# A four-layer graph attention kernel: tile 0 of the second layer computed densely, dense passes by halves of the heads, masks gathered as whole rows

## The chip, the cores and the metric

The kernel runs on one core of one Trainium2 chip. Time is device microseconds of an execution, here the median of three runs. The engines in the profile are PE (TensorE), DVE (VectorE), ACT (ScalarE), POOL (GpSimd) and SP (SyncE, which issues plain DMAs). Each has its own instruction queue and works it off in order; semaphores tie the queues together.

## The reference

Four graph attention layers run on 3327 nodes with 512 features and one symmetric adjacency matrix that holds about 16 neighbours per node, the node itself included. In each layer

```
h = relu(layernorm(x))
V = h W                                   # H heads of D = 512 / H features
e[i, j] = leaky_relu(s_i + d_j, 0.2)      # s, d: V times two vectors, per head
alpha = softmax over the neighbours j of i
x = x + act(sum_j alpha[i, j] V[j])       # act: elu in layers 1 and 2, else identity
```

with H = 8, 4, 1 and 8 heads in layers 0, 1, 2 and 3. (Below, "layer 1" is the second layer.) The nodes are padded to 26 tiles of 128.

## The kernel before, in words

**Preparation.** For each of the 26 row tiles the kernel loads the adjacency rows, finds each node's neighbours (up to 40, as sorted indices `L`), ranks the nodes by degree, and computes layer 0's rows of V (264 columns in each of two halves of the heads: 256 features and 8 score columns). Rows go to a table in DRAM: `tabx` for layer 0 (V and x side by side), `tab0` and `tab1` in turn for the others. The last part sorts nodes by degree into tiles: tile 0 holds the nodes with most neighbours. `CAPS` gives each tile's number of neighbour columns, from 36 (tile 0) down to 11 (tile 25), 467 in all. `Slots` holds the table indices of every tile and column. If the graph doesn't fit these caps, another branch (`tile_gat_dense`) runs; it didn't here.

**Lists.** In `tile_gat_lists` most tiles are computed from lists. A step is a group of up to four columns of one tile. `Tile.fetch` (L784 inside `gather`) issues one indirect DMA on POOL per column, which brings 128 table rows of 2112 B; in layers 1 to 3 the tile's own row comes through SP from `own_d` (L815). `scored` adds the scores and takes the exp (L839 to L842). `group` multiplies every gathered row by its weight on DVE (L865, 128x512) and adds the products up on PE with an identity matmul (L870, two records per product). In layer 2, with its one head, DVE does both (L858, L860) and PE is left to the dense passes. `finish` divides by the sum of weights, and `ends` lays out what follows over the next steps: `bent` (elu on ACT, L893 and L895), `added`, `centre`, `root`, `turn` (transposes, L451), `cut` (relu out of PSUM, L458), `project` (L469), `rows` (scaling, L476, and a write to `own_d`), and `scatter` (L792, one indirect DMA on POOL per tile).

**Dense passes.** The tiles of highest degree can be computed against all 26 source tiles j instead: a weight for every pair of nodes, times a mask, times V. `DENSE = [0, 0, 9, 2]` says how many tiles that is per layer. In layer 2 `Wholes` takes tiles 0 to 8 in three passes of three. In layer 3 `Several` takes tiles 0 and 1 with all 8 heads: for each j it loads 264 KB of the table (`ve`) and a mask (`mk`), ACT turns the mask into bf16 (L1157), PE copies it to PSUM (L1159), ACT computes three exps (L1161 to L1165) and eight Relus (L1171), DVE scales the features (`features`, L1176) and masks the weights (`masked`, L1185, two of 1024 elements), and PE multiplies (`products`, L1197).

**Masks.** They are made in layer 0 for tiles 0 to 8. A `Mask` step gathers half an adjacency row per node (6656 B, two gathers per tile), ACT makes it bf16 (L983), PE transposes it in pieces of at most 7 blocks (L989), ACT writes bytes (L995) and SP stores them.

**Order.** The order of PE, DVE, ACT and POOL is written by hand (`manual_schedule`). The loop over steps s runs `fetch` for the step that lies LOOK = 7 ahead, then the pieces registered by `later` for "first", then `scored` of step s + 1, the pieces for "scored", `group` of step s, and the pieces for "last". Tiles go from 25 down to the lowest list tile, and `place` spreads the pieces of the dense passes over the steps. `gpool` has seven buffers of four gathered rows, `mpool` three. In PSUM each tile of layers 0, 1 and 3 takes two banks of pool "o" in turn (four buffers): one for its sum `po`, one for its weights `pw`. Pool "t" (transposes) has two buffers in layers 0 and 1.

## Time and profile before

| | |
|---|---|
| median of three runs | 3105.87 us (3096.56 to 3113.53) |
| the profiled execution's own time | 2579.0 us |
| its span | 2577.0 us, mean granted clock 0.934 |
| preparation, up to the first gather | 274 us |
| layer 0, first to last gather | 274 to 925 us |
| layer 1 | 957 to 1530 us |
| layer 2 | 1560 to 2010 us, then a tail to 2050 us |
| layer 3 | 2051 to 2556 us |
| gathers and scatters of layers 0, 1 and 3 (POOL instructions) | 510, 457 and 406 |
| bytes moved | 613.85 MB, mean 238 GB/s |

The profiled execution is 527 us shorter than the median of the runs, which carry no trace. All rows of the trace belong to the shorter one.

How to read the trace: one row is a group of instructions of one line, with its engine, operation and tiles (out<-in), their number, busy time and mean duration; after a bar comes the idle time of the engine just before them and who ended it. "issue" stands for a wait that the profile shows no other engine for. A matmul's own duration overlaps with its neighbours', so a run of them is priced by the length of the run. Layers were cut by the times of their first and last gathers.

### The profile page before, as it was taken

What the parts mean: (1) busy time and instruction counts of PE and PEld (TensorE: products, weight loads), DVE (VectorE), ACT (ScalarE), POOL (GpSimd) and SP (SyncE); (2) the same over time, 40 slices, a digit from 0 to 9 for tenths busy, and PEclk for the clock granted to TensorE, in tenths of its full rate; (3) what the DMA queues carried; (4) which work ended last, traced back from release to release, by engine and by line L of the source; (5) the groups of instructions that cost most, each with busy time, mean ns of one, the idle gap of its engine ahead of it and who ended that gap; (6) DMA issues with size and microseconds to landing.
All of it is one profiled execution on the core that took longest, in us unless ns stands there. A gap on an engine that the chain in (4) does not pass through costs nothing. (4 is left out here: it accounts for less than half of the span.)

```text
span 2577.0 us, 25558 instructions
## 1 busy us (share of the span) xinstructions
PE 2113.2 (82%) x6708; PEld 1154.2 (45%) x6708; DVE 1965.1 (76%) x5080; ACT 756.5 (29%) x1827; POOL 1806.9 (70%) x1818
## 2 busy tenths in 40 slices
PE   3677799988988858998898986768787599998988
PEld 2566345444434424544444432435443445454543
DVE  8988887776666637888777765897989488878777
ACT  4876033223222201222211112343342322222221
POOL 6996477777777747777777764665656277777775
PEclk7898899999999989999999997888898799999999
DMA  5884688888888858888888785886878288888886
GB/s 227 306 321 177 193 257 265 267 282 262 262 266 259 244 155 236 247 243 240 237 236 238 235 220 191 262 251 222 253 234 249 99 251 245 250 243 243 242 239 178
DMA packets 234928, 613.85 MB, mean 238 GB/s; under 512 B 79059, under 2 KB 83155, under 8 KB 231446
## 3 DMA queue, kind: packets, MB, share of 16 engines
q0 software_dynamic: 135216, 464.80, 60.2%
q1 hardware_dynamic: 95814, 140.54, 16.1%
q10 hardware_dynamic: 3744, 6.82, 0.8%
q8 instruction: 54, 0.88, 0.1%
q14 instruction: 100, 0.82, 0.1%
HBM read 545.12 MB, written 66.89 MB: 237 GB/s over the span
## 5 line engine op out<-in xcount | busy, mean ns | idle before, releaser
L870 PE MATMUL bank<-m,ident 128*128 128x512 f32 x2680 | 1253.3, 615 | 201.6 <-DVE m L865 179.2
L865 DVE TENSOR_TENSOR m<-g,bank 128x512 f32<-128x512 f32 x1340 | 832.4, 681 | 103.5 <-ACT bank L842 97.9
L784 POOL DMA_INDIRECT g<-tab,idxb x769 | 733.0, 953 | 251.9 <-issue 180.5
L870 PEld LDWEIGHTS bank<-m,ident 128*128 128x128 f32 x2680 | 500.8, 195 | 836.8 <-DVE m L865 399.1
L469 PE MATMUL pv<-w,hT 128*128 128x264 f32 x1664 | 430.6, 415 | 80.9 <-ACT hT L458 58.1
L469 PEld LDWEIGHTS pv<-w,hT 128*128 128x128 f32 x1664 | 335.8, 205 | 183.8 <-ACT hT L458 73.4
L842 ACT ACTIVATE bank<-z 128x32 f32<-128x32 f32 (+4 forms) x371 | 71.8, 194 | 1169.4 <-DVE z L841 1169.1
L784 POOL DMA_INDIRECT g<-tabx,twiceb x342 | 324.5, 949 | 104.2 <-issue 78.6
L784 POOL DMA_INDIRECT g<-tab,idxa x297 | 282.7, 952 | 106.6 <-issue 69.5
L1076 PE MATMUL whole<-ve,em 128*128 128x512 f32 x468 | 224.5, 631 | 27.3 <-DVE em L1062 26.6
L839 DVE TENSOR_TENSOR z<-g,bank 128x32 f32<-128x32 f32 (+4 forms) x371 | 65.2, 176 | 217.5 <-DMA g<-tabx,twiceb 84.4
L628 POOL TENSOR_TENSOR key<-a,keys 128x3328 int32<-128x3328 int32 x26 | 189.3, 7290 | 4.3 <-DMA a<-in_adj 3.4
L860 DVE SCALAR_TENSOR_TENSOR bank<-g,pw,bank 128x512 f32<-128x512 f32 x243 | 183.2, 754 | 6.8
L1076 PEld LDWEIGHTS whole<-ve,em 128*128 128x128 f32 x468 | 92.4, 202 | 135.5 <-issue 105.1
L635 DVE MAX8 cand<-key 128x8 f32<-128x208 int32 x416 | 143.7, 364 | 0.6 <-POOL key L628 0.6
L451 PE MATMUL pt<-ident,xn 128*128 128x128 f32 x416 | 69.3, 293 | 88.1 <-ACT hT L458 36.1
L784 POOL DMA_INDIRECT g<-tabx,twicea x99 | 95.0, 960 | 61.7 <-issue 26.8
L792 POOL DMA_INDIRECT tab<-v,idxb x54 | 53.7, 994 | 101.9 <-ACT v L476 86.7
L451 PEld LDWEIGHTS pt<-ident,xn 128*128 128x128 f32 x416 | 53.4, 150 | 132.9 <-issue 44.5
L1197 PEld LDWEIGHTS whole<-vs,em 128*128 128x128 f32 x832 | 101.1, 189 | 25.0 <-issue 23.8
L1051 ACT ACTIVATE r<-low,mc,b 128x384 f32<-128x384 f32 x78 | 52.6, 675 | 167.7 <-DVE em L1062 150.9
L1197 PE MATMUL whole<-vs,em 128*128 128x130 f32 x832 | 101.4, 274 | 0.0
(168 smaller groups left out, 1920.3 us busy)
## 6 DMA issues: line engine op xcount, KB each, us to landing
a<-in_adj SPq DMA_DIRECT2D x26, 1664.0 KB, 9.3
ve<-tab SPq DMA_DIRECT2D x104, 264.0 KB, 4.5
own<-v SPq DMA_DIRECT2D x78, 264.0 KB, 3.8
g<-own SPq DMA_DIRECT2D x67, 264.0 KB, 4.1
tabx<-vx SPq DMA_DIRECT2D x26, 528.0 KB, 3.9
g<-tab,idxb POOLq DMA_INDIRECT x769, 3.9
vx<-in_x ACTq DMA_DIRECT2D x26, 256.0 KB, 2.8
g<-tabx,twiceb POOLq DMA_INDIRECT x342, 4.1
```

The lines of the kernel that those rows point to most:

```text
L451: nc.tensor.transpose(pt[:, k, :], xn[:, k * P:(k + 1) * P], ident)
L469: nc.tensor.matmul(pv[:, s, :HF + 8], hT[:, k, :], W.w[:, k, s, :], start=(k == 0), stop=(k == KC - 1))
L628: nc.gpsimd.tensor_tensor(key, a, keys, OP.mult)
L635: nc.vector.max(cand[:, g * 8:(g + 1) * 8], key[:, g * SEG:(g + 1) * SEG])
L784: nc.gpsimd.indirect_dma_start(out=out_, out_offset=None, in_=table, in_offset=bass.IndirectOffsetOnAxis(ap=which, axis=0))
L839: nc.vector.tensor_tensor(z, g[:, :n, ROW - 8:ROW - 8 + H], self.s.unsqueeze(1).to_broadcast([P, n, H]), OP.add)
L842: nc.scalar.activation(self.wt[:, k0:k0 + n, :H], z, AF.Exp)
L860: nc.vector.scalar_tensor_tensor(acc, v, w, acc, OP.mult, OP.add)
L865: nc.vector.tensor_tensor(m[:, q, :].rearrange("p (s h d) -> p s h d", s=2, d=D), v.rearrange("p s (h d) -> p s h d", d=D), wt[:, k0 + q, ...
L870: nc.tensor.matmul(self.po, ident, m[:, q, :], start=(k0 + q == 0), stop=(k0 + q == K - 1))
L1076: nc.tensor.matmul(tl.po.rearrange("p (s m) -> p s m", s=2), e[:, q * P:(q + 1) * P], v.rearrange("p (s m) -> p s m", s=2)[:, :, :F // 2], ...
L1197: nc.tensor.matmul(dst, e[:, h - 4 * half, q * P:(q + 1) * P], mov, start=False, stop=(j == NT - 1), skip_group_check=True)
```

## The change

It has these parts.

1. `DENSE[1]` becomes 1: in layer 1 tile 0 is no longer gathered column by column but goes through `Several`, with masks that exist already.
2. `Several` is rewritten. A unit is one source tile j and one half of the heads (2 of 4 in layer 1, 4 of 8 in layer 3), so a layer has 52 units; all 26 j of the upper half come first. Each unit loads its half of the table rows (132 KB) and the mask (16 KB for one tile, 32 KB for two). ACT writes the Relus into PSUM (`r`, one buffer) and scales the features, one instruction per head; DVE multiplies by the mask's bytes as they are, so that the bf16 mask and its copy by PE fall away. Loads are issued three units ahead. Its buffers are cut (`Room`) out of `low`, `L` and `spare`, which lie free after the preparation, and, for two tiles, one more.
3. A mask step gathers the whole adjacency row (13312 B) of each node into `low`: one gather per tile, steps 11 apart instead of 7 per half; one conversion of 3328 elements; four pieces of turning, whose copies stand in "last" instead of "scored".
4. PSUM: pool "o" has two buffers and holds only sums; weights lie in banks of their own, two in layer 0, and the two halves of one in layers 1 and 3. Pool "t" has one buffer.
5. `cut` moves from ("scored", b + 3) to ("last", b + 2), just after `turn`; in layer 2 `rows` moves from b + 5 to b + 4. `place` gets n - 8 steps instead of n - 6.
6. `Own` is for a dense tile in layer 0 and isn't used with this `DENSE`.

The diff, cut to its core:

```diff
-DENSE = [0, 0, 9, 2]
+DENSE = [0, 1, 9, 2]
...
-                                    (b + 2, "first", self.turn), (b + 3, "scored", self.cut),
-                                    (b + 3, "last", self.project), (b + 5, "scored", self.rows),
+                                    (b + 2, "first", self.turn), (b + 2, "last", self.cut),
+                                    (b + 3, "last", self.project), (b + 5 - (HEADS[self.l] == 1), "scored", self.rows),
...
     class Mask:
...
         def fetch(self):
-            n = NP // 2
-            g = gpool.tile([P, GROUP, ROW], F32, name="g")
-            self.a = g.rearrange("p q n -> p (q n)")[:, :n].bitcast(I32)
-            if self.side:
-                nc.scalar.activation(odd[:, self.t:self.t + 1], slots(self.t, 0, twice=True), AF.Copy, bias=1.0)
-            gather(self.a, adj.rearrange("r (s n) -> (r s) n", s=2),
-                   odd[:, self.t:self.t + 1] if self.side else slots(self.t, 0, twice=True))
+            self.a = low.bitcast(I32)
+            gather(self.a, adj, slots(self.t, 0))
...
         def finish(self, s):
-            for i, (c0, c1) in enumerate([(0, 7), (7, NT // 2)]):
+            for i, c0 in enumerate(range(0, NT, 7)):
+                c1 = min(c0 + 7, NT)
                 later(s + 1 + i, "first", self.turn(c0, c1))
-                later(s + 1 + i, "scored", self.keep(c0, c1))
+                later(s + 1 + i, "last", self.keep(c0, c1))
...
     class Several:
...
-        def features(self, j):
-            H, D, n = self.H, self.D, self.n * P
-            v = self.v.pop(j).rearrange("p (s m) -> p s m", s=2)[:, :, :F // 2]
-            nc.vector.tensor_tensor(
-                self.vs[j % 2][:, :H * (D + 1)].rearrange("p (s h d) -> p s h d", s=2, d=D + 1)[:, :, :, :D],
-                v.rearrange("p s (h d) -> p s h d", d=D),
-                self.k[j][:, n:n + H].rearrange("p (s h) -> p s h", s=2).unsqueeze(3).to_broadcast([P, 2, H // 2, D]),
-                OP.mult)
+        def load(self, u):
+
+            if u < 2 * NT:
+                i, j = divmod(u, NT)
+                table = tabs[self.l % 2] if self.l > 0 else tabx
+                c0 = (1 - i) * (ROW // 2)
+                nc.sync.dma_start(self.v[u % 3], table[j * P:(j + 1) * P, c0:c0 + ROW // 2])
+                nc.sync.dma_start(self.mk[u % 3], masks[0][j, :, :self.n * P])
+
+        def weights(self, u):
+
+            if u == 2 * NT:
+                return
+            i, j = divmod(u, NT)
+            n, Q, H, D = self.n * P, self.Q, self.H, self.D
+            if i == 0:
+                d = self.v[u % 3][:, ROW // 2 - 8:ROW // 2 - 8 + H]
+                nc.scalar.activation(self.b[:, j, :], d, AF.Exp, scale=1.0 - SLOPE)
+                nc.scalar.activation(self.c[:, j, :], d, AF.Exp, scale=SLOPE)
+            r = pools["r"].tile([P, self.n, BANK], F32, name="r").rearrange("p a b -> p (a b)")
+            self.r = r[:, :Q * n].rearrange("p (h c) -> p h c", h=Q)
+            for h in range(Q):
+                g = (1 - i) * Q + h
+                nc.scalar.activation(self.r[:, h, :], self.a[:, g, :], AF.Relu, bias=-1.0,
+                                     scale=self.b[:, j, g:g + 1])
+
+        def features(self, u):
...
+            for h in range(Q):
+                nc.scalar.activation(vs[:, h, :D], self.v[u % 3][:, h * D:(h + 1) * D], AF.Copy, scale=c[:, h:h + 1])
+            nc.scalar.activation(vs[:, :Q, D], c, AF.Copy)
+
+        def masked(self, u):
+            Q, n = self.Q, self.n * P
+            nc.vector.scalar_tensor_tensor(self.e[u % 2], self.r, 1.0,
+                                           self.mk[u % 3].unsqueeze(1).to_broadcast([P, Q, n]), OP.add, OP.mult)
...
+        def place(self, s0, s1):
+
+            later(s0 - 1, "first", self.begin)
+            for u in range(3):
+                later(s0 - 1, "first", lambda u=u: self.load(u))
+            later(s0 - 1, "scored", lambda: (self.weights(0), self.features(0)))
+            for u in range(2 * NT):
+                s = s0 + u * (s1 - s0) // (2 * NT)
+                later(s, "first", lambda u=u: self.masked(u))
+                later(s, "scored", lambda u=u: (self.weights(u + 1), self.features(u + 1), self.load(u + 3)))
+                later(s + 1, "first", lambda u=u: self.products(u))
+                if u % NT == NT - 1:
+                    later(s + 1, "last", lambda u=u: self.means(u // NT))
...
-            pools = {"o": pool("ps_o", 1 if whole else 4, **psum)}
+            pools = {"o": pool("ps_o", 1 if whole else 2, **psum)}
             if l < NL - 1:
-                pools.update(t=pool("ps_t", 1 if whole else 2, **psum))
+                pools.update(t=pool("ps_t", 1, **psum))
...
+                pools.update(p=pool("ps_p", 1 if DENSE[l] else 2, **psum))
                 if DENSE[l]:
-                    pools.update(w=pool("ps_w", 3, **psum), k=pool("ps_k", 1, **psum), e=pool("epool", 1))
+                    pools.update(w=pool("ps_w", l // 3 + 1, **psum), r=pool("ps_r", 1, **psum))
...
             if l == 0:
-                for i, (t, side) in enumerate(itertools.product(range(ND), range(2))):
-                    steps.insert(12 + 7 * i, (Mask(t, side), 0))
-            if DENSE[l]:
-                wholes.place(len(steps) - 6)
+                for t in range(ND):
+                    steps.insert(18 + 11 * t, (Mask(t), 0))
...
+            if whole:
+                wholes.place(len(steps) - 8)
+            elif DENSE[l]:
+                wholes.place(32 if l == 0 else 0, len(steps) - 8)
```

## Prediction

> **What bounds the kernel now.** I read the page first (busy shares, then the groups), next the busy times cut at the layers' edges, then the waits of layer 1, and last the instructions around layer 2's end. The page's first part says only that no engine is full, because it averages over stages:
>
> ```profile
> span 2577.0 us, 25558 instructions
> PE 2113.2 (82%) x6708; PEld 1154.2 (45%) x6708; DVE 1965.1 (76%) x5080; ACT 756.5 (29%) x1827; POOL 1806.9 (70%) x1818
> ```
>
> Cut at the layers' edges (start:end, length, then PE, PEld, DVE, ACT, POOL busy with instructions, granted clock, DMA share, GB/s; the rows are layers 0, 1, 2, the gap after 2, and 3):
>
> ```profile
> 274.00:930.00 656.00, 570.18 (x1702) 284.57 (x1702) 465.53 (x1232) 160.34 (x349) 485.91 (x510) 0.96 0.85 256
> ...
> 956.00:1530.00 574.00, 505.34 (x1381) 254.14 (x1382) 438.89 (x1165) 113.06 (x297) 434.38 (x457) 0.97 0.80 237
> ...
> 1560.00:2010.00 450.00, 335.46 (x948) 186.08 (x948) 371.54 (x711) 161.31 (x395) 271.07 (x287) 0.86 0.76 239
> 2010.00:2050.00 40.00, 24.99 (x96) 19.06 (x96) 14.13 (x33) 12.05 (x24) 7.55 (x9) 0.83 0.18 68
> 2050.00:2560.00 510.00, 462.85 (x1690) 252.71 (x1691) 408.03 (x847) 130.45 (x428) 385.44 (x406) 0.98 0.82 243
> ```
>
> POOL looks like the third engine, but divide length by its instructions: 574/457 = 1.256 us in layer 1, 510/406 = 1.256 us in layer 3. A constant pitch through tiles of 11 and of 36 columns means that something issues without pause. The waits of layer 1 (total, times, longest) say what:
>
> ```profile
> POOL g L784 <- issue: 97.8, 321, 0.3
> ```
>
> The longest is 0.3 us and no engine is awaited: each gather is 0.95 us and is followed by a fixed 0.30. So POOL's issue of indirect DMAs, 1.25 us each, sets layers 0, 1 and 3; its 75.6% is its ceiling. PE is next (505 of 574 = 88% in layer 1). Layer 2 is different: DVE has 372 of 450 there, and a tail in which it has ended and nothing is gathered:
>
> ```profile
> 2022.66 0.75 DVE L883 TENSOR_SCALAR low<-bank,den 128x512 f32<-128x512 f32 x1
> ...
> 2028.29 0.60 ACT L458 ACTIVATE hT<-pt 128x512 f32<-128x512 f32 x1 [3.98 <-PE pv L469]
> ...
> 2034.04 0.62 ACT L893 ACTIVATE neg<-low 128x512 f32<-128x512 f32 x1
> ...
> 2047.41 1.03 POOL L792 DMA_INDIRECT tab<-v,idxb  x1 [6.32 <-ACT v L476]
> ```
>
> The last tile's mean is ready at 2023.4, yet ScalarE takes it up at 2034.0: in its order three hT and three v of earlier tiles stand ahead, most of them waiting for a PE projection. That is 10.6 us on the path.
>
> **What the Trainium skill says.** *DMA: Bandwidth & Descriptors*, SWDGE vs HWDGE vs iDMA: descriptors of a DMA issued on GpSimd are generated in software on its cores. The trace agrees that the price is per gather, not per byte: 0.942 us for a half adjacency row (6656 B), 0.943 for a double table row (4224 B), 0.953 for one row (2112 B). *ScalarE: Activation LUTs*, What ACT_TABLE_LOAD costs: 186 ns + 0.833 ns per element, 93 more for a pointer operand, 93 of overlap between neighbours. The trace has 495 ns for the 256-wide Relu of L1171 (the formula gives 493); I use it for widths that the trace lacks. *PSUM — Partial Sum Buffer*, bank collisions: two engines must not touch one bank at once. This bears on the two tiles' scores that now share a bank; the trace already shows m waiting 0.3 us for the next group's exp in its own bank.
>
> **The change, part by part** (against the profiled execution: 2579.0 us, of it 2577.0 span).
>
> 1. *Layer 1, tile 0 without lists.* POOL loses 35 gathers (36 columns; the own row came through SP): 35 x 1.25 = 43.8 us on the path. What is late next? PE: out go 36 x 2 records at 0.43 (8 in 3.43 us on the chain) = 30.9; in come 52 units x 2 heads x 2 records at 0.112 (16 in 1.79) = 23.3, zeroing 2 banks 1.7, targets 2.1. So 505.3 - 30.9 + 27.1 = 501.5 in 574 - 44 = 530, 94.6%. The stretch 1000 to 1100 us already has 94.4% PE with POOL at full pitch, so I keep the gain, minus 3 us for the first small tiles, where PE's work per tile is about POOL's time. DVE: out 36 x 0.62 = 22.3, nine groups of z 3.1, divisors 1.2; in 52 masked products of 256 elements at 0.49 (line through 384 at 0.610 and 1024 at 1.211) = 25.5: level, 439 of 530. ACT: per unit two Relu and two scalings of 128 (387 - 93 = 294 ns each, estimate from the ScalarE page), two copies or exps of about 0.2: 1.6, so 83; 113 + 83 - 2 = 194 of 530, covered. SP gets 104 loads at 0.32 us of issue, three units (some six steps of 5 us) ahead against 3.6 to 4.5 us to landing; behind them stand the own-row loads, with seven steps of lead. Bytes: 36 x 264 KB = 9.5 MB out, 52 x (132 + 16) KB = 7.7 MB in. **-41 us.** Ends: -44 if PE never stops POOL; about -4 if PE keeps all of its 69 idle us (501.5 + 69 = 570).
>
> 2. *Masks from whole rows (layer 0).* Eighteen gathers become nine: 9 x 1.25 = 11.3 us. No row shows a gather of 13312 B per partition. From below 0.95, since three sizes up to 6656 B cost alike; from above twice that, if it cost like two halves, with nothing gained. I take 0.95, for the three rows are flat. The same bytes in bigger lumps make list rows behind them land late: the 1664 KB loads of the same rows land in 9.3 us, the halves in 6.8; POOL, up to seven steps ahead, doesn't wait for landing. ACT's conversion is one piece of about 3 us instead of two of 1.58, with a step of 5 us as cover; uncovered, 9 x 1.5 = 14 us. One PSUM buffer for turning instead of two makes PE wait for ScalarE's copy (0.9 us) when a mask and a tile turn in one step; PE's 13% of idle covers it. **-11 us.**
>
> 3. *Layer 3 by halves.* POOL's list is unchanged, 406 instructions: **0**. DVE loses 26 x 0.685 = 17.8 us, PE 26 k products (7.1), ACT gains 26 x 2 x (4 x 0.24 + 0.19) - 26 x 0.6 = 44 (24%), none of it on the path at 80%, 91% and 26%. ACT's old wait for PE's k (67.8 us in all) goes too, into idle time. SP gets 52 more issues. Uncovered, ACT's 44 is the loss.
>
> 4. *Layer 2's order.* cut follows turn in the same step, rows come a step earlier, and the dense passes are placed over n - 8 steps instead of n - 6: the last pass ends at step 60 instead of 63, while the last list tile still finishes at 71. In the changed order only one v stands between ScalarE's last exp and the last neg, where there were three hT and three v. Of the 10.6 us I take 9, as that v may wait for PE. DVE has the same work. Ends: 0 to -13 (with part of PE's 21.5 us of waits for hT inside the layer). **-9 us.**
>
> 5. *Scores in halves of one bank (layers 1 and 3).* At each of 49 tile changes m or exp may wait 0.3 us: 15 us in all, hidden in DVE's idle time (91 us left in layer 1, 120 in layer 3): 0, at most 15. The zero column, Room and the idle class Own: 0.
>
> Sum -41 - 11 + 0 - 9 = -61: the profiled execution should go from 2579 to about 2518. The median, 3105.87, is 527 us (1.204 times) above that execution and the page doesn't say where they lie. I subtract the sum unscaled: 3106 - 61 = **3045 us**; scaled it is 73 and 3033.
>
> **Rivals.**
> - *PE takes over in layer 1*: for it, 94.6%; against it, the stretch with 94.4% at full pitch. -4 - 11 - 9 = -24: 3082.
> - *The unprofiled time stretches POOL's issue*, or layer 2 gives its 13 as well: -73 to -92: 3014 to 3033, say 3030.
> - *The extra 527 us belong to something that the change doesn't relieve* (DMA time: layer 1 loses 1.8 MB, layer 3 gains 0.8 in shorter rows): only the tail remains, 3097. The profile can't speak against it.
> - *Slower: ScalarE's new bundle* (1.6 us per unit in layer 1, 2.9 in layer 3: Relus, scalings, copies) stands in one queue ahead of the next group's exp, and scaling waits for PE to leave vs. An exp has one step, 5.0 us, of lead; from a bundle plus wait above 5 us on, every unit stops m, and with it the buffers that gathers need. If half of each bundle shows, 52 x 0.8 + 52 x 1.45 = 117: 3106 - 61 + 117 = 3162. Against it: ACT at 37% and 34%, and m's own buffers bind on PE first.
>
> **How the numbers follow.** Forecast 0.50 (own range 3033 to 3058); stretched POOL 0.14; PE 0.16; unrelieved 0.12; slower 0.08. A measurement of this kernel can tell about 0.5% (15.5 us) from no change. Faster 0.50 + 0.14 + 0.16 = 0.80, same 0.12, slower 0.08. The range runs from 3012 (stretched) to 3090 (PE rival with the mask gather at double price, which returns another 11) and leaves out the last two.
>
> **What would show it.** Layer 1 near 533 us with some 422 POOL instructions at a pitch of 1.256; a pitch of 1.33 or more there and POOL waiting for DVE m means PE took over. Layer 0 some 11 us shorter, nine gathers into low at about 0.95 us; 1.9 would refute step 2. Layer 3 at 510 with ACT near 175. Between DVE's last mean in layer 2 and the next gathers about 19 us instead of 28. I am wrong if POOL gets waits longer than 0.3 us in layers 0, 1 or 3, or if profile and median move by different amounts.

## The result and the profile after

The changed kernel takes 2982.15 us (2978.08 to 2986.43, four runs), the kernel before 3108.05 beside it: ratio 0.960, interval 0.957 to 0.963, a gain of 126 us. I had forecast 3045, a gain of 61. The sign was right and the gain was twice what I had summed.

The profiled execution of the changed kernel took 2978.08 us, as long as its other runs, while that of the kernel before, from which my sum was made, took 2579.0. The experiments point to the reason: **the two traces were taken on chips of two kinds.** On four of the chips used below the kernel before takes 2578 to 2587 us, on three others 3105 to 3124, and on each of them its profiled execution, where it was taken, agrees with its other runs. I call them quiet and stopping chips, for a reason that follows. By its time, the trace of before belongs to the first kind; the forecast's runs and the trace of after belong to the second. Which chips these first runs had is not on record, and each later chip was used for one group of runs only, so it stays open whether the kind belongs to the chip or to the time of the runs. So the trace of after answers to mine only through two more traces: after on a quiet chip (e3) and before on a stopping one (e14).

The first part of the page, after on the forecast's chip:

```profile
span 2976.4 us, 26618 instructions
...
PE 2249.4 (76%) x6832; PEld 1233.1 (41%) x6832; DVE 1939.2 (65%) x5056; ACT 890.3 (30%) x2321; POOL 1771.0 (60%) x1774
```

POOL has lost 44 instructions, 35 gathers and nine halves of masks, as summed. But POOL is now at 60% where before it was at 70%. Busy times cut at the layers' edges show where the span went (start:end, length, then busy us and instructions of PE, PEld, DVE, ACT, POOL, granted clock, DMA share, GB/s; rows are layers 0 to 3). First a quiet chip, the kernel before (e4), then after (e3), on the same one:

```profile
275.00:949.00 674.00, 586.03 (x1740) 292.64 (x1740) 474.02 (x1259) 163.29 (x355) 485.93 (x510) 0.96 0.83 250
956.00:1569.00 613.00, 531.91 (x1454) 269.12 (x1454) 455.40 (x1205) 118.56 (x309) 443.99 (x467) 0.97 0.78 228
1572.00:2045.00 473.00, 350.24 (x1024) 199.34 (x1024) 382.99 (x730) 170.47 (x413) 277.29 (x295) 0.88 0.73 230
2048.00:2567.00 519.00, 470.68 (x1708) 255.78 (x1708) 414.21 (x859) 130.54 (x429) 386.40 (x407) 0.98 0.80 240
```
```profile
273.00:938.00 665.00, 582.88 (x1740) 294.38 (x1740) 474.32 (x1260) 162.13 (x337) 477.06 (x502) 0.96 0.83 253
945.00:1512.00 567.00, 515.07 (x1604) 280.89 (x1604) 447.37 (x1202) 200.19 (x613) 410.94 (x432) 0.98 0.81 244
1516.00:1972.00 456.00, 347.76 (x1029) 196.39 (x1027) 383.40 (x730) 170.46 (x415) 277.20 (x294) 0.87 0.76 239
1978.00:2498.00 520.00, 462.32 (x1652) 246.30 (x1652) 402.67 (x837) 179.15 (x632) 388.86 (x407) 0.98 0.81 241
```

Then the stopping chips, the kernel before (e14), then after (the forecast's own run):

```profile
277.00:1105.00 828.00, 626.17 (x1740) 311.18 (x1740) 472.54 (x1259) 161.53 (x355) 485.45 (x511) 0.88 0.69 203
1113.00:1848.00 735.00, 572.84 (x1454) 286.59 (x1454) 453.15 (x1205) 119.69 (x309) 442.37 (x466) 0.88 0.66 190
1852.00:2355.00 503.00, 365.55 (x1024) 203.58 (x1024) 383.57 (x730) 170.83 (x413) 277.55 (x295) 0.85 0.70 216
2358.00:3105.00 747.00, 531.43 (x1708) 281.23 (x1708) 415.56 (x859) 130.43 (x429) 386.59 (x408) 0.84 0.57 166
```
```profile
276.00:1104.00 828.00, 622.49 (x1740) 311.43 (x1738) 472.01 (x1260) 162.04 (x337) 477.54 (x501) 0.88 0.68 203
1112.00:1823.00 711.00, 562.96 (x1604) 298.85 (x1604) 447.10 (x1202) 201.43 (x613) 409.86 (x431) 0.89 0.67 195
1827.00:2312.00 485.00, 358.04 (x1030) 201.36 (x1029) 383.83 (x730) 170.32 (x413) 278.31 (x294) 0.86 0.73 224
2318.00:2972.00 654.00, 519.60 (x1652) 272.89 (x1652) 398.86 (x837) 180.97 (x632) 390.32 (x408) 0.86 0.66 191
```

Read the lengths, and then how little the busy times of DVE, ACT and POOL differ between the kinds of chip: the work is the same, only the waiting and TensorE's clock are not. From the exact start of each layer's first gather to that of its last scatter (a little more than the front's cut, which ends with the gathers):

| us | quiet: before | after | gain | stopping: before | after | gain | forecast |
|---|---|---|---|---|---|---|---|
| layer 0 | 674.1 | 664.5 | 9.6 | 827.8 | 828.3 | -0.5 | 11 |
| layer 1 | 612.5 | 566.8 | 45.7 | 735.9 | 711.3 | 24.6 | 41 |
| layer 2 with its tail | 472.3 | 456.6 | 15.7 | 502.6 | 485.6 | 17.0 | 9 |
| layer 3 | 518.6 | 520.5 | -1.9 | 746.1 | 653.9 | **92.2** | 0 |
| preparation and joints | 289.6 | 289.8 | -0.2 | 292.3 | 292.4 | -0.1 | 0 |

The gains add up to 69 us on the quiet chip, where the timed runs give 70, and to 133 on the stopping ones, where they give 126 (the two traces there are of two chips). So my sum holds where its trace came from, and most of what it missed lies in **layer 3**, which I had put at nothing.

**What a stopping chip does.** First what POOL waits for in layer 1 of after, on the forecast's chip and then on the quiet one (total, times, longest):

```profile
POOL g L786 <- issue: 109.7, 347, 1.1
...
POOL g L786 <- DVE m L865: 42.8, 21, 9.1
```
```profile
POOL g L786 <- issue: 93.5, 307, 0.3
```

On the quiet chip no "issue" wait of a gather exceeds 0.3 us, as before the change, and the gathers keep their pitch of 1.258 us; on the other the pitch is 1.55 us. There POOL stands up to 9.1 us behind DVE's m, which is what I had named as the sign that I am wrong. Behind DVE's waits stands TensorE, often by way of ScalarE: in layer 3 of after, on the forecast's chip, DVE's m waits for ScalarE's exp up to 25.7 us, and ScalarE's scaling of the features for TensorE's products up to 12.0. TensorE's matmul records in that layer, on the same chip (start, length, instruction, idle before it):

```profile
2776.26 1.02 PE L1233 MATMUL whole<-spare,low 128*128 128x130 f32 x7
2779.81 0.77 PE L870 MATMUL bank<-m,ident 128*128 128x512 f32 x1 [2.53 <-issue]
2783.31 1.01 PE L870 MATMUL bank<-m,ident 128*128 128x512 f32 x1 [2.73 <-issue]
2785.41 1.01 PE L870 MATMUL bank<-m,ident 128*128 128x512 f32 x1 [1.08 <-issue]
2787.50 1.01 PE L870 MATMUL bank<-m,ident 128*128 128x512 f32 x1 [1.09 <-issue]
```

Records that follow each other in 0.43 us elsewhere start 3.50, 2.10 and 2.09 us apart: multiples of 0.70, with "issue", no other engine, as their releaser. I call this a stop: for some 12 us TensorE starts only four of these records, and then goes on. The granted clock follows it (start:end, length, then the columns as above):

```profile
2777.00:2780.00 3.00, 0.47 (x3) 0.20 (x2) 2.93 (x7) 0.00 (x0) 2.18 (x3) 1.00 0.83 227
2780.00:2789.00 9.00, 3.70 (x5) 0.96 (x4) 1.04 (x3) 2.03 (x5) 4.52 (x5) 0.51 0.71 209
```

In the first 3 us TensorE is busy for 0.47 and the clock is still 1.00; only then does it fall. In layers 0 and 3 of this trace gathers start over 4 us apart about every 30 us (28 times in 828 us, 20 in 654); on the quiet chip once and never. Counting sequences of at least four TensorE records (products and weight loads) that start 0.70 us or a small multiple apart gives 19 in the after trace, 12 in e14's and 24 in e16's; in each of the traces from quiet chips, none. The count finds the long, regular stops only.

Why I don't take the half clock for the cause: the Trainium skill, *TensorE: Matmul & The Clock Gate*, Part 1 (The HAM clock gate), says that the array falls to half clock after an idle window of about 3.4 us, and that its activity gate knows half and full clock only. The traces agree: their clock records hold 0.5 and 1.0 alone, in pieces of 3.41 us or a multiple (but for the last, which the end of the trace shortens). e5, with fewer products, fell from 0.938 to 0.872 without losing time, so a low mean clock alone is no loss. And imposed stops make layer 3's gain on a quiet chip whose mean clock is 0.95 (e7 and e8 below). How much of the longer time on a stopping chip the half clock adds was not separated.

### The profile page after: what moved, and what is told of

It reads as the page before. It is cut to its first block, busy times and chain, and to the rows that moved or that the text cites. A ratio compares the mean times of both kernels' runs of the same rounds, so it can differ in the third digit from the quotient of the medians.

```text
span 2976.4 us, 26618 instructions
## 1 busy us (share of the span) xinstructions
PE 2249.4 (76%) x6832; PEld 1233.1 (41%) x6832; DVE 1939.2 (65%) x5056; ACT 890.3 (30%) x2321; POOL 1771.0 (60%) x1774
## 5 line engine op out<-in xcount | busy, mean ns | idle before, releaser
L870 PE MATMUL bank<-m,ident 128*128 128x512 f32 x2608 | 1320.9, 655 | 322.3 <-DVE m L865 189.4
L865 DVE TENSOR_TENSOR m<-g,pw 128x512 f32<-128x512 f32 x1304 | 810.9, 681 | 535.3 <-ACT pw L842 309.4
L870 PEld LDWEIGHTS bank<-m,ident 128*128 128x128 f32 x2608 | 525.9, 209 | 973.8 <-issue 631.1
L786 POOL DMA_INDIRECT g<-tab,idxb x734 | 701.7, 956 | 376.5 <-issue 199.8
L469 PE MATMUL pv<-w,hT 128*128 128x264 f32 x1664 | 450.7, 429 | 82.3 <-ACT hT L458 42.4
L842 ACT ACTIVATE pw<-z 128x32 f32<-128x32 f32 (+5 forms) x434 | 83.3, 192 | 878.1 <-DVE z L841 454.4
L839 DVE TENSOR_TENSOR z<-g,pw 128x32 f32<-128x32 f32 (+5 forms) x434 | 74.3, 171 | 102.8 <-DMA g<-tab,idxa 63.0
L458 ACT ACTIVATE hT<-pt 128x512 f32<-128x512 f32 x104 | 61.1, 588 | 200.0 <-remote 111.6
L476 ACT ACTIVATE v<-pv,rstd 128x528 f32<-128x528 f32 x78 | 54.2, 695 | 210.7 <-PE bank L870 104.5
L1210 ACT ACTIVATE spare<-room,low 128x64 f32<-128x64 f32 x208 | 57.8, 336 | 183.8 <-remote 81.7
```

Source lines behind the costliest of these rows:

```text
L458: nc.scalar.activation(hT, pt, AF.Relu)
L469: nc.tensor.matmul(pv[:, s, :HF + 8], hT[:, k, :], W.w[:, k, s, :], start=(k == 0), stop=(k == KC - 1))
L786: nc.gpsimd.indirect_dma_start(out=out_, out_offset=None, in_=table, in_offset=bass.IndirectOffsetOnAxis(ap=which, axis=0))
L839: nc.vector.tensor_tensor(z, g[:, :n, ROW - 8:ROW - 8 + H], self.s.unsqueeze(1).to_broadcast([P, n, H]), OP.add)
L842: nc.scalar.activation(self.wt[:, k0:k0 + n, :H], z, AF.Exp)
L865: nc.vector.tensor_tensor(m[:, q, :].rearrange("p (s h d) -> p s h d", s=2, d=D), v.rearrange("p s (h d) -> p s h d", d=D), wt[:, k0 + q, ...
```

## Experiments

**e0, e4, e11, e14: the kernel before again,** for its trace on other chips. No edit.

> The kernel before, unchanged, for a second trace beside its median of 3108. Theory A (one of two courses of the same program was caught in the first trace, and timed executions take the other): this trace has a span near 3100, and layers 0, 1 and 3 are longer in it while the preparation is the same, about 274 us. Theory B (the 527 us lie outside the span, ahead of the first or after the last instruction): the span is again near 2577.

> The kernel before, unchanged, for its trace on the chip of this call. Theory A: if it takes about 3100 us here, the granted clock in layers 0, 1 and 3 is 0.86 to 0.89 instead of 0.96 to 0.99, half-clock spells sum to over 700 us instead of 340, and the gathers' pitch is 1.25 us outside the stalls that follow those spells; if it takes about 2587, the clock is near 0.93 again. Theory B (the lost time is in DMA or in POOL's issue): at 3100 us the pitch of the gathers is longer everywhere, or the DMA's packets take longer.

> The kernel before, unchanged, on the chip of this call, for its trace. On a chip where it takes about 3106 us: TensorE's stops of 4 to 16 us (records 0.70 us apart or a multiple of it) appear in layers 0, 1 and 3 about every 28 us, as in after's forecast trace, and half-clock time is over 750 us; if they came from the changed kernel alone, they are missing here. On a chip where it takes about 2580: no such records, and a clock near 0.93.

> The kernel before, unchanged, for its trace. On a slower chip (about 3110 us): TensorE's stops as in the changed kernel's forecast trace, but more of them or longer, since the clock of its runs there (0.85 to 0.87) stands for 810 to 940 us of half clock against 758 in the changed kernel; layer 1, where the change takes 72 accumulation records out, should hold the larger part of the extra 56 us. If the stops cost both alike, each layer is longer by the same factor, 1.18 to 1.2, and the extra is spread. On another chip: 2575 to 2590 us and no stops.

Measured 2588.3 (clock 0.937), 2576.5 (0.936), 2581.8 (0.937) and 3113.8 us (0.859). The first three are quiet chips. Profiled executions and timed ones take the same on all four, so a profile doesn't shorten a run, and I take the 527 us that I had called unprofiled for the difference between two kinds of chip. The e14 trace has the stops in the kernel before too, so they aren't brought by the change. It refutes two guesses of its expectation: the extra gain is neither in layer 1 nor spread evenly.

**e1: after with tile 0 of layer 1 in lists; e2: after with masks from half rows.**

```diff
-DENSE = [0, 1, 9, 2]
+DENSE = [0, 0, 9, 2]
```
```diff
...
-                for t in range(ND):
-                    steps.insert(18 + 11 * t, (Mask(t), 0))
+                for i, (t, side) in enumerate(itertools.product(range(ND), range(2))):
+                    steps.insert(12 + 7 * i, (Mask(t, side), 0))
```

> The changed kernel with DENSE = [0, 0, 9, 2]: tile 0 of layer 1 is in the lists again, all other parts of the change stay. Theory P (the gain is the 35 gathers and their work that layer 1 loses, and POOL or PE sets it): this kernel gives back most of the 126 us, some 44 to 75, so 3026 to 3057. Theory Q (the gain is in the order and the PSUM pools, which let the queues wait less for one another in all layers): it gives back 10 to 35 only, 2992 to 3017, and layers 0 and 3 stay as in the changed kernel.

> The changed kernel with masks gathered as two half rows again (18 gathers into the ring of seven buffers, 18 conversions, steps 7 apart; the copies stay in last). Theory P (POOL's issue sets layer 0): +11 us, 2993. Theory Q (POOL isn't the bound in the timed course): within 10 us of 2982, or more than +25 if the mask steps take buffers from the ring that the lists need.

Measured on one quiet chip, against 2587.3: e1 2560.6 (ratio 0.990, 0.987 to 0.993), e2 2523.5 (0.977, 0.974 to 0.980). By layers, e1 has layer 1 at 614.4, so tile 0 is worth 47 us against e2's 567.5 on the same chip (48 against e3's 566.8). e2 has layer 0 at 676.4, so whole rows are worth 10 us against e1's 666.7 (12 against e3's 664.5). In e1's time all parts but tile 0 together give 27 us, the whole rows included.

**e3: after itself on a quiet chip; e5 and e15: after with fewer accumulations; e6: with more.** e5 and e15 leave out about half of the columns of the sums and e6 counts some twice, so their output is not the layer's; only their time is used. The edit of e5 and e15:

```diff
             for q in range(n):
+                if q % 2 and k0 + q < K - 1:
+                    continue
                 nc.tensor.matmul(self.po, ident, m[:, q, :], start=(k0 + q == 0), stop=(k0 + q == K - 1))
```

> The changed kernel itself, beside the kernel before on one chip. Theory A (my sum was right for a chip on which POOL's issue is the bound, and the extra gain of the forecast runs belongs to a chip whose TensorE clock is throttled more): where the kernel before takes about 2587 us with a granted clock of 0.93, after takes 2515 to 2525 (e2, all but the whole-row masks, was 2523.5, and nine gathers less are worth up to 11 us: 2513), so a gain of 62 to 75 us; where the kernel before takes about 3106 us, after takes about 2982, a gain of about 125, at a clock near 0.87 for both. Theory B (the extra gain is a property of the change and not of the chip): a gain of about 125 us on any chip.

> After, with every second accumulation by the identity matrix (line 870) left out in layers 0, 1 and 3, so those sums lack about half of their columns; DVE's products, gathers and everything else stay. TensorE loses about half of 1304 accumulations of 0.86 us, some 540 us of 2250 (2100 on the faster chip). Theory A (TensorE's throttled clock is what stops the buffers, and then POOL): on a throttled chip the time falls from 2980 to 2500 or less, and half-clock time to under 350 us; on the faster chip it falls from 2518 to 2470 to 2500 (stalls of TensorE in layer 1 go, POOL's 1.25 us pitch stays). Theory B (DMA or POOL): within 1% of after on either chip.

> After, with the first accumulation of each group of four columns (line 870) done twice in layers 0, 1 and 3, so those sums count some columns twice; about 330 more accumulations of 0.86 us, 280 us more for TensorE and nothing more for any other engine. Theory A: TensorE becomes the bound on any chip; on the faster chip the time goes from 2518 to 2700 or more, with more half-clock time, and POOL waits for DVE's m in stalls of some us, as on the throttled chip. Theory B: TensorE's idle time (17 to 24% of the span) takes most of it, and the time rises by under 100 us.

> The changed kernel with every second accumulation by the identity matrix (line 870) left out in layers 0, 1 and 3, as in e5. On a slower chip: if the stops follow TensorE's work (its load over some tens of us), they nearly vanish, and the time falls from 2980 to 2510 to 2600; if they come at fixed times whatever TensorE does, it stays above 2800. On another chip: 2507 us as e5, since TensorE isn't the bound there.

e3 took 2508.9 us, ratio 0.973 (0.969 to 0.976), a gain of 70 us: theory A's side, though below its 2515 to 2525. e5 (one run) took 2507.4, nothing less, though TensorE's busy time fell from 2089 to 1810: on a quiet chip TensorE isn't the bound, and A's 2470 to 2500 was too low. e6 (one run) took 2623.0: 245 us more of TensorE cost 114, between both theories, so the margin is thin there. e15 (one run), on a stopping chip, took 2932.8 against after's 2982 on the forecast's. TensorE was busy for 1894 us instead of 2249, and POOL still stood idle for over 4 us 66 times in the four layers, 67 times in after (11 in e3): the stops stayed with a sixth less work on TensorE, so the claim that they nearly vanish with its load fell.

**e7 and e8: both kernels with imposed stops; e12 and e13: with longer ones.** Products of a column of zeros are added to the group's bank, so sums stay as they are.

```diff
...
+            if 0 < k0 and next(beat) % 5 == 4:
+                for _ in range(7):
+                    nc.tensor.matmul(self.po, ident, zero.to_broadcast([P, F]), start=False, stop=False)
             for q in range(n):
...
```

e12 and e13 have 14 products there, and seven more in layer 2's dense passes:

```diff
...
+                for _ in range(7 if j % 5 == 2 and q == 0 else 0):
+                    nc.tensor.matmul(tl.po, ident, zero.to_broadcast([P, F]), start=False, stop=False)
```

> The kernel before with stops put into TensorE: in layers 0, 1 and 3, ahead of every fifth group's accumulations (about every 25 us), seven products of a column of zeros are added to the group's bank, 14 matmul records of 0.43 us, 6 us each; 59 such bursts, 354 us of TensorE. It imitates what the trace of the slower chip shows, where TensorE nearly stops for 4 to 16 us about every 28 us in those layers. Theory A (what the slower chip adds is TensorE's stops, which POOL cannot make up at a pitch of 1.25 us, and the changed kernel can absorb more of them because its layer 1 has fewer of the products that wait): on a chip where before takes 2580, this takes 2800 to 2930, and e8 gains 90 us or more on it. Theory C (stops cost both kernels alike, and the 126 us are the chip's longer time with nothing of the change in it): the gap to e8 is 70 us, as without bursts, plus at most the 12 us of the two bursts fewer.

> After with the same bursts (57 of them, 342 us). Theory A: 2700 to 2820 on a chip where after takes 2509, and a gain of 90 us or more on e7, towards the 126 of the forecast's chip. Theory C: a gain of 70 to 82 us on e7.

> The kernel before with stops twice as long: in layers 0, 1 and 3 fourteen added products of zeros (12 us) at every fifth group, 59 of them, and in layer 2 seven (6 us) at every fifth neighbour block of each dense pass, 15 of them; 800 us of TensorE in all. Theory A (stops cost the kernel before more once they are as long as the slower chip's): 3050 to 3200, and over 100 us more than e13. Theory D (stops of a given number and length cost both alike, and TensorE then sets the time, where the two kernels differ by 26 us of busy time and two stops): 30 to 75 us more than e13.

> After with the same long stops (57 of 12 us and 15 of 6 us, 774 us of TensorE). Theory A: 2930 to 3080, over 100 us less than e12. Theory D: 30 to 75 us less than e12, of it up to 24 from the two stops fewer.

Measured 2746.1 and 2684.3 us (quiet chip), 3354.7 and 3267.4 (this one a stopping chip, before 3123.8). All four totals miss what I expected, and so do the gaps: 62 us lies under theory C's 70 to 82, 87 us between D's 75 and A's 100. Cut by layers, in one trace each, they say more:

| us | e7 | e8 | gap | e12 | e13 | gap |
|---|---|---|---|---|---|---|
| layer 0 | 712.3 | 717.4 | -5 | 906.2 | 928.8 | -23 |
| layer 1 | 654.4 | 647.5 | 7 | 805.3 | 805.6 | 0 |
| layer 2 | 475.3 | 460.9 | 14 | 525.8 | 522.0 | 4 |
| layer 3 | 603.2 | 565.4 | **38** | 823.9 | 717.4 | **107** |

The more TensorE stops, the less the change gains in layers 0 and 1, where POOL's list no longer sets the time, and the more it gains in layer 3. So theory A fails for the whole kernel: by the totals the stops of e7 and e8 cost the kernel before 167 us and the changed one about 175 (2684.3 less e3's 2508.9, on another quiet chip). In layer 3 alone they cost the kernel before more. There DVE's wait for ScalarE's k grows in the kernel before with the stops: 18 us in all on a quiet chip (e4), 88 in e7, 202 in e14, 230 in e12, where the change gains -2, 38, 92 and 107 us.

**e9: three tiles without lists in layer 3; e10: dense passes over n - 6 steps.**

```diff
-DENSE = [0, 1, 9, 2]
+DENSE = [0, 1, 9, 3]
```
```diff
...
-                wholes.place(len(steps) - 8)
+                wholes.place(len(steps) - 6)
```

> After with three tiles instead of two without lists in layer 3. POOL loses the 22 gathers of tile 2, 27.5 us at 1.25; TensorE gains 52 units x 4 heads x 2 records x 0.112 = 47 and loses 23 x 2 x 0.43 = 20, so 454 + 27 = 481 of the 473 us that POOL's list would then leave in layer 3. If TensorE takes over there, as one of my rivals had it for layer 1: -15 to +20 us against after; if not: -27. Against the kernel before a ratio of 0.963 to 0.98.

> After with layer 2's dense passes placed over n - 6 steps again instead of n - 8; cut and rows stay as after has them. If the place is what opens the queue at layer 2's end (my step 4): the gap between layer 2's last DVE mean and layer 3's first gathers grows by some 5 to 9 us and the time rises to 2514 to 2520 against 2509 where before takes 2579. If cut and rows did it: within 3 us of after, a ratio of 0.972 to 0.974 to before. On a chip where before takes 3106: about 2990.

e9 took 2489.8 us, ratio 0.966 (0.964 to 0.969): layer 3 at 494.5 instead of 520.5, 26 of the 27.5 us of POOL's gathers. It beats both kernels on a quiet chip; on a stopping one it wasn't run. e10 took 2507.3, ratio 0.972 (0.970 to 0.975): after's time, with layer 2 at 460.3 us, where traces with n - 8 have 456.6 (e3) to 461.9 (e1). But its trace has the queue at layer 2's end back:

```profile
1957.11 0.75 DVE L883 TENSOR_SCALAR low<-bank,den 128x512 f32<-128x512 f32 x1
...
1969.30 0.62 ACT L893 ACTIVATE neg<-low 128x512 f32<-128x512 f32 x1
...
1985.17 1.00 POOL L786 DMA_INDIRECT g<-tab,idxa  x1 [2.62 <-issue]
```

ScalarE takes the last mean up 11.4 us after its end, and the next gathers come 27.3 us after it, as in the kernel before (e4: 12.2 and 27.6; e3: 0.03 and 18.0). In return the last mean is ready sooner: 436.7 us after the layer's first gather, against 444.0 in e3 and 448.5 in e4. So the place does open the queue, as my step 4 had it, and pays for it inside the layer; it is worth little or nothing. By elimination the gain, some 12 us in e10, comes from the order of cut and rows. TensorE's waits for ScalarE's hT in layer 2 point the same way: 63 us in e4, 25 in e10, 27 in e3. Which of the two moves does it wasn't separated.

**e16: the kernel before without TensorE's k in layer 3; e17: the same with the stops of e7.**

```diff
...
-            mk = self.mk[j] = pools["e"].tile([P, self.n * P], U8, name="mk", bufs=2)
+            mk = self.mk[j] = pools["e"].tile([P, self.n * P], U8, name="mk", bufs=3)
...
-            real = pools["e"].tile([P, n], BF16, name="real", bufs=2)
-            nc.scalar.activation(real, self.mk.pop(j), AF.Copy)
-            k = self.k[j] = pools["k"].tile([P, BANK], F32, name="k")
-            nc.tensor.matmul(k[:, :n], ident_b, real, start=True, stop=True)
+            k = self.k[j] = pools["e"].tile([P, 8], F32, name="kf", bufs=3)
...
-                                           self.k[j][:, :n].unsqueeze(1).to_broadcast([P, 4, n]), OP.add, OP.mult)
+                                           self.mk[j].unsqueeze(1).to_broadcast([P, 4, n]), OP.add, OP.mult)
```

> The kernel before with one part of the change alone, in layer 3: TensorE's product k (line 1159), which brought the mask into a PSUM bank, and ScalarE's conversion ahead of it are gone; the mask is read by DVE as it was loaded, and the factors of the features lie in SBUF; DVE still scales the features. Nothing else differs. If TensorE's k in DVE's path is what made layer 3 longer under TensorE's stops: on a slower chip (before about 3110 us) 40 to 95 us less than before, layer 3 at 650 to 705 instead of 746; on another chip within 10 us of before (2579), layer 3 near 519. If something else of the change did it (ScalarE's scaling, halves, fewer DVE instructions): within 15 us of before on either chip.

> The same edit with the bursts of e7 (59 stops of 6 us). Layer 3 was 603 us in e7 (kernel before) and 565 in e8 (changed kernel), on a chip that stops little by itself. If k in DVE's path is the cause: layer 3 at 560 to 580 and about 2710 to 2725 in all on such a chip, against e7's 2746; if not: layer 3 at 595 to 605 and 2740 to 2750.

Against "nothing else differs", the edit also gives the mask a third buffer, and the factors, which shared k's one bank, three buffers of their own in SBUF. Both runs fell on a stopping chip. e16 took 3007.3 us against 3105.2: ratio 0.967 (0.960 to 0.974), 98 us, just beyond the 40 to 95 that I expected. By layers it is e14, on another stopping chip, with one number changed:

```profile
281.00:1106.00 825.00, 626.39 (x1740) 307.95 (x1740) 472.88 (x1259) 161.92 (x355) 485.93 (x510) 0.88 0.69 204
1113.00:1846.00 733.00, 573.06 (x1454) 286.03 (x1454) 453.20 (x1205) 119.47 (x309) 442.70 (x466) 0.88 0.66 191
1850.00:2352.00 502.00, 364.18 (x1024) 204.04 (x1024) 383.72 (x730) 170.81 (x413) 277.59 (x295) 0.84 0.70 217
2355.00:3000.00 645.00, 504.75 (x1682) 278.07 (x1682) 412.30 (x859) 119.46 (x402) 408.96 (x407) 0.86 0.66 193
```

Layer 3 is 645 us where e14 has 747 and after 654. Twenty-six products of 0.27 us (median; 0.42 at most) and as many conversions of 0.40, taken out of the path, are worth the whole of layer 3's gain; ScalarE's scaling, the halves and DVE's 17.8 us are not needed for it. Of the edit's own parts the extra buffers are the untested rival. The e14 trace speaks against them: ScalarE's conversion of the mask never waits there, and TensorE waits 6.5 us in all just ahead of its 26 products k, none of it for DVE or ScalarE to leave the bank. On a quiet chip the edit wasn't run. e17 took 3071.6, with layer 3 at 671.9; its counterpart e7 ran on a quiet chip, so it decides nothing.

How so small an instruction does that is to be seen in e14, the kernel before, at one stop in layer 3:

```profile
2493.24 0.40 ACT L1157 ACTIVATE real<-mk 128x256 bf16<-128x256 uint8 x1
...
2496.68 1.01 PE L870 MATMUL bank<-m,ident 128*128 128x512 f32 x1 [1.51 <-issue]
...
2499.47 1.01 PE L870 MATMUL bank<-m,ident 128*128 128x512 f32 x1 [1.78 <-issue]
...
2508.34 0.42 PE L1159 MATMUL k<-real,ident_b 128*128 128x256 bf16 x1
...
2508.80 0.18 ACT L1161 ACTIVATE k<-ve 128x8 f32<-128x8 f32 x1 [15.16 <-PE k L1159]
...
2509.01 0.69 DVE L1176 TENSOR_TENSOR vs<-ve,k 128x512 f32<-128x512 f32 x1 [13.20 <-ACT k L1161]
```

The mask is converted at 2493.6. Its product stands in TensorE's queue behind accumulations that a stop spreads over 14 us. ScalarE waits 15.16 us for it: its exps don't use the mask, but their factors go into the same bank. DVE waits 13.20 us for ScalarE, and behind DVE's `features` stand the m of the list tiles. So after the stop TensorE soon runs out of m and stands a second time: 1.02 us at this stop, 169 us in 23 waits over layer 3. DVE's waits over layer 3, e14 and then the same kernel on a quiet chip:

```profile
DVE vs L1176 <- ACT k L1161: 201.8, 22, 13.2
```
```profile
DVE vs L1176 <- ACT k L1161: 18.4, 11, 3.6
```

In after there is no such product. DVE reads the mask as it was loaded, and the idle time of TensorE for DVE's m in layer 3 falls from 169 us (e14) to 16; in e16 it is 12. Its "issue" waits there rise at the same time, from 39 us to 112 and 120, so the stops themselves stay.

## Why the prediction missed

1. *Layer 1, tile 0: -41.* Right on a quiet chip: layer 1 gains 46, and tile 0 alone is worth 47 or 48 (e1). On the stopping chip it is 25. POOL waits there for DVE's m (42.8 us in layer 1), so a gather less need not save its whole pitch; that this is the difference was not tested. It lies between my -41 and the -4 of "PE takes over".
2. *Masks: -11.* Right on a quiet chip, 10 to 12 us. The undetermined price is settled in both traces of after, 0.946 us here (e3) and 0.949 on the forecast's chip:

```profile
L786 POOL DMA_INDIRECT low<-in_adj,idxb x9 | 8.5, 946 | 2.7 <-issue 1.5 <-DMA g<-tabx,twiceb 0.9 <-PE pv L469 0.3
```

 That is for 13312 B per partition, as I took it from the flat rows. (The section of the Trainium skill that the forecast names for this tells only who makes the descriptors; that the price doesn't depend on the bytes is shown by these rows alone.) On the stopping chip layer 0 gains nothing: POOL's pitch is 1.59 us there, so its issue no longer sets the time.

3. *Layer 3 by halves: 0.* **This is the step that failed.** I costed it on POOL's unchanged list and wrote that ACT's wait for PE's k, 67.8 us, "goes too, into idle time". On the trace's chip that is so: layer 3 is 2 us longer. On stopping chips, the kind of the timed runs, it is -92, and e16 shows -98 for the k product with its conversion and bank alone. I had looked at how long the chain PE to ACT to DVE waits, not at what it does when TensorE is late. The wait of my "slower" rival is there as well: on the forecast's chip ScalarE's scaling (L1210) stands for 184 us in layer 3, on the quiet one (e3) for 1.6. It costs less than k's product did: layer 3 is 654 us in after and 645 in e16, where DVE scales.

4. *Layer 2's order: -9.* 16 on the quiet chip and 17 on the other. The sign is right; that the size is near is in part luck, since the gain isn't where I put it. After on the quiet chip:

```profile
1958.85 0.75 DVE L883 TENSOR_SCALAR low<-bank,den 128x512 f32<-128x512 f32 x1
1959.63 0.63 ACT L893 ACTIVATE neg<-low 128x512 f32<-128x512 f32 x1 [2.30 <-DVE low L883]
...
1972.12 1.03 POOL L794 DMA_INDIRECT tab<-v,idxb  x1 [7.14 <-ACT spare L1167]
1977.56 0.98 POOL L786 DMA_INDIRECT g<-tab,idxa  x1 [4.41 <-issue]
```

 ScalarE takes the last mean up 0.03 us after its end, where it had left it for 10.6; from the start of that mean to the next gathers it is 18.7 us, as forecast (19). But e10 leaves the queue at the end as it was and has the same time. What shortens the layer lies inside it, in TensorE's waits for hT, of which I had taken a part only for the far end of my range.

5. *Scores in halves of a bank: 0.* Nothing in layers 1 and 3 of the quiet chip speaks against it.

Two figures of my working don't follow from its sums: the range's ends lie 2 and 3 us below them (3106 - 92 = 3014, 3082 + 11 = 3093), and the 24% beside ACT's 44 us fits none of its figures (174 of 510 us are the 34% of the rivals).

The second fault lies beside step 3: **I subtracted a sum made on one execution from the median of runs that took 527 us longer,** unscaled, on the thought that the missing time touched nothing. Of the 126 us, 70 is what the trace could tell, and the quiet chip gives them. The rest comes from waits that it didn't show, with opposite signs: about 30 us less in layers 0 and 1, about 94 more in layer 3. The rival "the extra 527 us belong to something that the change doesn't relieve" had the right question and the wrong answer.

What starts a stop, and why some chips have them and others don't, is not settled. The change doesn't bring them (e14). POOL's issue and DMA don't look longer with them: one gather of `tab` takes 0.953 us in e4 and 0.952 in e14, and the packets of the gathers' queue take 60.4% of 2574 us in e4 and 50.9% of 3112 in e14, 1555 and 1584 us. e15 shows that a sixth less work on TensorE doesn't end them.

## What to carry to other kernels

Where the profiled execution and the timed runs differ by a fifth, have both kernels traced on a chip like that of the timed runs before pricing a step at nothing: the bound can be another one. A small product that stands in TensorE's queue and that two other engines wait for can cost little while TensorE is on time and a multiple of itself when it is late: here 26 products and 26 conversions, some 18 us together, were worth 98 us. Gathers taken from a list that issues without pause gained their pitch where nothing else made that list wait, and about half of it where something did. And when a wait disappears in a trace, look whether the stretch as a whole got shorter: in layer 2 the place took 9 us off the end and put most of it back inside.

## What was unexpected of the hardware

- One and the same kernel takes 2578 to 2587 us on four chips and 3105 to 3124 on three others, steadily while it was measured there (2575 to 2590 in seven runs on e3's chip, 3087 to 3135 in seven on e16's). DVE's, ScalarE's and POOL's durations hardly differ: m takes 0.680 us in e4 and 0.682 in e14, a Relu of 256 columns 0.495 in both, a gather of `tab` 0.952 to 0.972 on three of the chips.
- On the stopping chips TensorE's records come 0.70 us or a multiple apart for 2 to 20 us at a time (after, e14, e16). In e14 all twelve of these sequences start at full clock; the half clock follows 1.4 to 5.4 us later in eleven and 8.9 us later in one.
- On a stopping chip 800 us of added products of zeros cost the kernel before only 231 us, and its granted clock rose from 0.858 to 0.938 (e12).
